# Graph layer with top-p attention: the first row tile of the second step is guessed from 24 of 26 key tiles, and the work around the turn is regrouped

## The chip, the cores and the metric

The kernel runs on one core of one Trainium2 chip. The metric is device time in microseconds of one execution; several runs are given by their median. A profiled execution is one run of the same program with the hardware profiler on, and all rows come from such a run.

## The reference

There are N = 3327 nodes with 256 features. After a layer norm and a ReLU the layer makes two steps of two diffusions. One goes through a sparse random adjacency matrix (about four entries a row besides the diagonal), the other through attention that keeps, in every row, the largest probabilities up to a mass of 0.9:

```python
h = jnp.maximum(_layernorm(x, axis=-1), 0.0)
# attention of one step
q = X @ W1.T @ W2.T
k = X @ W3.T
probs = jax.nn.softmax(q @ k.T / TAU, axis=-1)
idx = jnp.argsort(-probs, axis=-1)
sp = jnp.take_along_axis(probs, idx, axis=-1)
cs = jnp.cumsum(sp, axis=-1)
keep_sorted = cs - sp < TOP_P          # TOP_P = 0.9
A = probs * mask
A = A / jnp.maximum(A.sum(-1, keepdims=True), 1e-12)
# two steps; R is the row-normalised adjacency plus the identity
for n in range(2):
    A = _top_p_attention(Xa, W1, W2, W3)
    Xf = R @ Xf
    Xa = A @ Xa
    Z = Z + Xf @ U1[n].T + Xa @ U2[n].T
```

The result is a layer norm of `X + Z`, added to x. What matters here: the second step's keys are made from the first step's result, so no row of the second step can be summed over all columns before the last row tile of the first step is done.

## The kernel before

The rows are cut into 26 tiles of 128 (3328 with one padding row). For each row tile, `weights` takes the queries from `project`, multiplies them with all keys on TensorE (PE, `pl`, L603) in four chunks of 832 columns (two halves of 416), and ScalarE (ACT) writes the exponentials into one of a few buffers of 128 x 3328 (L607, the last chunk L611 and L613), with their sums in `za`. Nothing is sorted. Instead the threshold of each row is guessed and then settled from a few candidates:

- `guessed` (L619 to L629) computes a first threshold on ACT from the row's sum Z and from the moments of its logits (`ms`). In the first step and for tiles 0 to 2 of the second these come from `moments` (L507) and `project` (L519); for the other tiles of the second step `laws` (L553) makes them in one go: PE L561, VectorE (DVE) L564 to L568, and operations over 23 columns on GpSimd (POOL), L572 to L579.
- `measured_once` (first step) or `measured_twice` (second) measures mass and count at that threshold by scans over the whole row on ACT (`ja`, L636; three scans in the second step) and corrects it, with single columns computed on DVE (L688, L689, L702, L703, L719, L720), POOL (L680, L681, L693 to L695, L700 to L715) and ACT.
- `settle` makes, on DVE, the masked row `w` with the mass below the guess (L734), takes the 8 largest of each of 20 segments (`cand`, L739), draws the largest 48 in six rounds (`bb`, L746, L748), finds by cumulated sums (L753 to L758) the last one that is kept, and writes the masked exponentials back into `e` (L768; L765 in two pieces for tiles 0 and 25).
- `prove` (L776) checks for a whole step, in small DVE operations on 26 columns, that the guesses left the answer inside the candidates. If they did not, a flag sends the program through the slow `search_graph_layer` afterwards.

The masked row is then transposed by PE (`pt`, L813), copied by ACT (`eT`, L815) and multiplied with the features on PE (`pa`, L827); `finish` ends the tile.

The adjacency part is sparse: `refetch` gathers the rows of `vx`, the first step's result in DRAM, with five indirect DMAs a tile that POOL issues (L906, `xg<-vx`); each gather waits for all writes to `vx`. `spread` and `diffuse` multiply them on PE into `pr` (L914), a PSUM buffer of which there is one, and DVE ends it (L1087, L1088); in the first step it then writes `vx` for its tile.

The outer loop runs over tiles `i` in each step. In one turn each running piece of work (a Python generator) is advanced in an order written out by hand: seven parts a turn, each part a string of letters in which `m` is the guess of the next tile, `d` the settling of this one, `c` the end of the settling before it, `s` a spread, `g` a refetch, `l` the laws, `w` and `q` the logits and queries of later tiles, `f` finish and `e` the end of the first step. PE, ACT and DVE execute in exactly this text order from the first turn on, POOL from the start of the second step on:

```python
PLAN = (("mdsssa", "mdsssa", "edawwp", "msda", "mpdea", "gdawwq", "emdgq"),
        ("llcmss", "lnms", "lwwnfd", "lcmdsssg", "fmswqdf", "llmdf", "lmwfd"))
```

At the turn between the steps (`step == 1 and i == -1`) the kernel completes the logits of tile 0, proves the first step, makes all laws, measures tile 0, and refetches the adjacency rows of tiles 0 and 1, all before tile 0 is settled. `moments(1)` and three projections follow the first step's turn `i == NT`. The spreads of tiles 24 and 25 of the first step stand in its turns `i == NT` and `NT + 1`.

Of the kernel before, what the change touches and what calls it, by code (L numbers as in the profile page):

```python
# [9 lines left out]
F32 = mybir.dt.float32  # L10
# [318 lines left out]
HALVES = 9  # L329
FIRST = 8 * P  # L330
CUT = 4

# [12 lines left out]
def guess_graph_layer(ctx, tc, x, adj, w1t, w2t, w3t, u1t, u2t, ln_g, ln_b, out, flag):  # L345
# [207 lines left out]
    def laws(ts):  # L553

        at = lambda k, a, b: law[:, k, a:b]
        few_of = [ts[h::2][n : n + 3] for n in range(0, len(ts), 3) for h in range(2)]
        for few in filter(len, few_of):
            pq = ps_t.tile([P, 4, P], F32, tag="pt", name="pq")
            pm = pq.rearrange("p a b -> p (a b)")[:, : 3 * (2 * DA + 2)].rearrange("p (t n) -> p t n", t=3)
            for k, t in enumerate(few):  # L560
                PE.matmul(pm[:, k, :], query_of(t), qm[query_at(t), 1, :], start=True, stop=True)  # L561
            wide = scan.tile([P, NP], F32, tag="w", name="wide")
            mq = wide[:, : 3 * (2 * DA + 2)].rearrange("p (t n) -> p t n", t=3)
            V.tensor_copy(mq[:, : len(few)], pm[:, : len(few)])  # L564
            V.tensor_copy(law[:, 2, few[0] : few[-1] + 1 : 2], mq[:, : len(few), DA])
            for k, t in enumerate(few):
                V.scalar_tensor_tensor(mq[:, k, : DA + 1], mq[:, k, : DA + 1], 1.0, mq[:, k, DA + 1 :],
                                       ALU.mult, ALU.mult, accum_out=at(1, t, t + 1))  # L568
            yield
        a, b = ts[0], ts[-1] + 1  # L570
        s, var, m = (at(k, a, b) for k in range(3))
        G.tensor_tensor(s, var, halves[:, a:b], ALU.pow)  # L572
# [12 lines left out]
    def weights(step, t, live, known=True):  # L585

        r = dict(Z=rec[:, step, 3, t : t + 1])
        qT, r["ms"] = yield from project(step, t, law=known and not step)
        if known and step:
            r["ms"] = law_of(t)  # L590
        yield
        r["ms"] = r["ms"] or early.get(t)
        r["e"] = e = es[(2, 3, 0, 1, 4, 5)[t % 6] if step else t % 4]
        r["za"] = za = small.tile([P, CUT + 1], F32, tag="za", name="za")
        live[step, t] = r
        w = HALF * P
        wd = w // CUT
        for n in range(CUT):
            c = n * wd
# [6 lines left out]
            if n < CUT - 1:  # L606
                S.activation(e.rearrange("p (a n) -> p a n", a=2)[:, :, c : c + wd], pl[:, :, :wd],  # L607
                             AF.Exp, accum_out=za[:, n : n + 1])
                yield
            else:  # L610
                S.activation(e.rearrange("p (a n) -> p a n", a=2)[:, :, c : w - 1], pl[:, :, : wd - 1],  # L611
                             AF.Exp, accum_out=za[:, n : n + 1])
                S.activation(e[:, w - 1 : w], pl[:, 0, wd - 1 : wd], AF.Exp, accum_out=za[:, n + 1 :])  # L613

# [16 lines left out]
    def con(k):  # L631
        return one[:, k : k + 1]
# [39 lines left out]
    def measured_twice(r):  # L672
# [46 lines left out]
        V.tensor_scalar(col(6), d1, col(0), BIG, ALU.is_lt, ALU.mult)  # L719
        V.tensor_scalar(col(16), col(3), col(13), col(6), ALU.mult, ALU.add)  # L720

    def measured(step, r):
        return measured_twice(r) if step else measured_once(r)

# [50 lines left out]

    def prove(step):  # L776
        v8, t, tn, Z = (rec[:, step, k, :] for k in range(4))
        ok = small.tile([P, NT], F32, tag="cum", name="ok", bufs=1)
        o2 = small.tile([P, NT], F32, tag="dr", name="o2", bufs=1)
        V.tensor_tensor(ok, v8, t, ALU.is_lt)  # L780
        V.tensor_tensor(o2, tn, t, ALU.is_lt)
        V.tensor_tensor(ok, ok, o2, ALU.mult)
        for a, c, op in ((tn, 0.0, ALU.is_gt), (t, 0.5 * BIG, ALU.is_lt),
                         (Z, 1.0e-30, ALU.is_gt), (Z, BIG, ALU.is_lt)):
            V.scalar_tensor_tensor(ok, a, c, ok, op, ALU.mult)
        V.tensor_scalar(ok, ok, 0.5, None, ALU.is_lt)
        n = N - (NT - 1) * P
        f = small.tile([P, 1], F32, tag="f", name="f")
        V.tensor_reduce(f, ok[:, : NT - 1], AX.X, ALU.add)
        V.tensor_tensor(fl, fl, f, ALU.add)  # L790
        V.tensor_tensor(fl[:n], fl[:n], ok[:n, NT - 1 :], ALU.add)
        if step == 0:
# [3 lines left out]
            V.tensor_tensor(fl, fl, f, ALU.add)  # L796
# [173 lines left out]
    def run(work, n=99):  # L970
        for _ in range(n):
            next(work, None)
# [141 lines left out]
    for step in range(2):  # L1114
        sums = Sums(step, live, xw if step else x0, AHEAD[step])

        for i in range(-1, NT + 2):
# [26 lines left out]
            if step == 0 and i >= NT - 2 and i < NT + 1:  # L1144

                work["w"] = itertools.islice(begun[i - NT + 2], CUT - 1)
            if step == 0 and i >= NT - 3 and i < NT:
# [2 lines left out]
                work["w"] = itertools.chain(begun[1], begun[2])  # L1150
            if step == 0 and i < 1:
                work["b"] = itertools.islice(product, EARLY[i + 2] - EARLY[i + 1])
            if step == 1 and i == -1:
                work["g"] = itertools.chain(refetch(0), refetch(1))
            for k in range(PARTS):
                g = PARTS * (i - 1) + k - LATE[step]
                summing = valid(g // PARTS)
                if summing and step:
                    sums.turn(g, min(i, NT - 1))
                for c in "bb" + (LAST.get(i, PLAN[1]) if step else PLAN[0])[k]:  # L1160
# [9 lines left out]
            if step == 1 and i == -1:  # L1170
                run(work["m"])
            if step == 0 and i == -1:
                G.memset(es[2][:, N:NP], 0.0)
            for c in "lcnwqsepgb" if step else "dmwqsepgb":
# [55 lines left out]
```

## Time and profile before

| quantity | us |
|---|---|
| median of 3 runs | 1430.68 (1430.28 to 1431.4) |
| the profiled execution, whole | 1432.74 |
| its span, first to last instruction | 1431.0 |
| PE busy | 1280.6 (89%) |
| DVE busy | 1221.3 (85%) |
| ACT busy | 1106.3 (77%) |
| POOL busy | 985.9 (69%) |
| keys of the second step complete (ACT L497) | 781.69 |
| w of tile 0, second step, begins (DVE L734) | 802.99 |
| e of tile 0 begins (DVE L765) | 826.58 |
| e of tile 1 begins (DVE L768) | 851.06 |

The mean granted PE clock is 0.965 of full speed. Times in rows count from the span's start. In a row of a timeline the first number is the start, the second the duration in us, then engine, line of kernel.py, operation, result and operands with their shapes; in brackets the engine's idle time before it and what ended it. A row may hold several instructions (x10). In the chain of waits each row is a piece of the chain that ended last: start, duration, engine, result and line.

### The profile page before, as it was taken

How to read it: one execution, taken by the hardware profiler on the slowest of the kernel's cores; microseconds unless marked ns; L12 is line 12 of the kernel's file. 1: busy time of each engine (PE TensorE's matmuls, PEld its weight loads, DVE VectorE, ACT ScalarE, POOL GpSimd, SP SyncE). 2: the span in 40 equal slices, each digit the busy share in tenths (PEclk: the TensorE clock that was granted, in tenths of full speed). 3: DMA queues.
4: the chain of work that ended last, by engine and by line, in shares of the span. 5: the costliest groups of instructions: out<-in, count | busy, mean ns of one | idle time of the engine just before them, and what ended most of it. 6: DMA issues, size and time to landing. Idle time of an engine off the chain costs nothing.

```text
span 1431.0 us, 22249 instructions
## 1 busy us (share of the span) xinstructions
PE 1280.6 (89%) x6495; PEld 980.6 (69%) x6495; DVE 1221.3 (85%) x3724; ACT 1106.3 (77%) x2426; POOL 985.9 (69%) x1348
## 2 busy tenths in 40 slices
PE   6987799999999999999999469999999999999846
PEld 4534587777777777777777247777776777777745
DVE  5676999999999999998872589999999999999980
ACT  5358588787887878788844789999999999999811
POOL 6035477677676677678862667888878888888731
PEclk9998899999999999999999679999999999999978
DMA  7873445454454545433331212222122221221100
GB/s 248 291 245 93 123 124 152 125 148 131 141 143 129 144 130 146 137 103 78 99 89 52 66 38 78 71 63 89 57 77 74 61 89 55 79 78 56 56 8 22
DMA packets 91203, 149.78 MB, mean 105 GB/s; under 512 B 15265, under 2 KB 58656, under 8 KB 91072
## 3 DMA queue, kind: packets, MB, share of 16 engines
q1 hardware_dynamic: 73616, 105.37, 23.6%
q0 software_dynamic: 16640, 42.69, 11.7%
q8 instruction: 54, 0.88, 0.3%
q14 instruction: 77, 0.63, 0.1%
q10 hardware_dynamic: 816, 0.20, 0.1%
HBM read 120.93 MB, written 27.28 MB: 104 GB/s over the span
## 4 chain that ended last, share of the span: by engine, by line
DVE 50%; PE 24%; ACT 16%; POOL 4%; issue 4%; DMA 2%; SPq 0%; POOLq 0%; DVEq 0%; ACTq 0%
ACT ja L636 10%; PE pa L827 10%; DVE e L768 10%; DVE cand L739 7%; DVE w L734 6%; DVE fm L849 5%; PE pl L603 4%; DVE bb L746 4%; DVE cand L748 4%; PE pt L813 3%; DVE x L768 2%; PE pz L991 2%; ACT eT L815 2%; POOL xg L906 2%; PE pr L914 2%
## 5 line engine op out<-in xcount | busy, mean ns | idle before, releaser
L827 PE MATMUL pa<-xw,eT 128*128 128x256 f32 x1352 | 332.5, 388 | 18.6 <-DVE s L938 18.4
L636 ACT ACTIVATE ja<-e,g 128x3328 uint8<-128x3328 f32 x106 | 325.9, 3074 | 0.1
L827 PE MATMUL pa<-x,eT 128*128 128x256 f32 x1352 | 324.8, 382 | 0.0
L827 PEld LDWEIGHTS pa<-xw,eT 128*128 128x128 f32 x1352 | 250.4, 192 | 80.2 <-issue 27.1
L815 ACT COPY eT<-pt 128x512 f32<-128x512 f32 (+1 forms) x364 | 202.1, 556 | 104.7 <-PE pt L813 104.5
L827 PEld LDWEIGHTS pa<-x,eT 128*128 128x128 f32 x1352 | 244.8, 192 | 26.2
L739 DVE MAX8 cand<-w 128x8 f32<-128x168 f32 (+1 forms) x1040 | 251.0, 317 | 0.0
L813 PE MATMUL pt<-ident,e 128*128 128x128 f32 x1144 | 182.0, 280 | 68.8 <-DVE e L768 47.4
L906 POOL DMA_INDIRECT xg<-bx,index x130 | 194.8, 1498 | 48.5 <-issue 37.6
L813 PEld LDWEIGHTS pt<-ident,e 128*128 128x128 f32 x1144 | 141.7, 145 | 115.8 <-issue 55.9
L897 POOL DMA_INDIRECT ac<-in_adj,index x130 | 133.6, 1028 | 120.7 <-DVE ms L541 83.9
L734 DVE SCALAR_TENSOR_TENSOR w<-e,g 128x3328 f32<-128x3328 f32 x44 | 168.9, 3838 | 0.7
L906 POOL DMA_INDIRECT xg<-vx,index x130 | 130.9, 1007 | 45.6 <-issue 33.0
L768 DVE SCALAR_TENSOR_TENSOR e<-e,rec 128x3328 f32<-128x3328 f32 x40 | 155.7, 3891 | 0.7
L914 PE MATMUL pr<-xg,ac 128*128 128x257 f32 (+1 forms) x520 | 139.4, 392 | 12.1 <-DVE s L1088 12.0
L607 ACT ACTIVATE e<-pl 128x832 f32<-128x832 f32 x132 | 112.8, 858 | 32.4 <-PE pl L603 32.3
L914 PEld LDWEIGHTS pr<-xg,ac 128*128 128x128 f32 x520 | 94.0, 195 | 25.8 <-DVE s L1088 12.1
L954 POOL TENSOR_TENSOR s<-s,gam 128x256 f32<-128x256 f32 x25 | 92.5, 3699 | 9.0 <-ACT s L953 9.0
L746 DVE MAX8 bb<-cand 128x8 f32<-128x160 f32 x286 | 92.8, 325 | 6.4
L603 PE MATMUL pl<-both,qT 64*128 64x416 f32 x416 | 93.0, 551 | 5.3 <-ACT e L607 3.8
L603 PE MATMUL pl<-after,qT 64*128 64x416 f32 x416 | 96.7, 559 | 0.6 <-ACT qT L531 0.6
L770 POOL TENSOR_TENSOR cum<-dr,bb 128x48 f32<-128x48 f32 x26 | 84.8, 3261 | 15.1 <-DVE rec L758 15.0
(259 smaller groups left out, 2193.8 us busy)
## 6 DMA issues: line engine op xcount, KB each, us to landing
at<-in_adj SPq DMA_DIRECT2D x102, 256.0 KB, 2.7
cx<-ac SPq DMA_DIRECT2D x26, 384.0 KB
ac<-cx SPq DMA_DIRECT2D x26, 384.0 KB, 3.0
wide<-in_adj SPq DMA_DIRECT2D x10, 832.0 KB, 6.6
e<-in_adj SPq DMA_DIRECT2D x8, 832.0 KB
bx<-e SPq DMA_DIRECT2D x26, 128.5 KB, 3.8
own<-bx SPq DMA_DIRECT2D x26, 128.5 KB, 3.3
x<-in_x SPq DMA_DIRECT2D x13, 256.0 KB, 5.0
```

What stands on the lines that cost most here:

```text
L603: PE.matmul(pl[:, a, :wd], qT[p, :], keys_of(step, a).rearrange("p a b -> p (a b)")[:, c : c + wd], start=True, stop=True)
L636: S.activation(ja, e, f, bias=guess, scale=sign, accum_out=total)
L734: V.scalar_tensor_tensor(w, e, col(16), e, ALU.is_lt, ALU.mult, accum_out=d2)
L739: V.max(cand[:, 8 * s : 8 * s + 8], w[:, s * SEG : min(NP, (s + 1) * SEG)])
L746: V.max(b8, cand)
L768: V.scalar_tensor_tensor(e, e, at(1), e, ALU.is_ge, ALU.mult, accum_out=ra)
L813: PE.transpose(pt[:, j, :], e[:, (j0 + j) * P : (j0 + j + 1) * P], ident)
L815: S.copy(eT[:, :w, :], pt[:, :w, :])
L827: PE.matmul(self.pa, eT[:, c - 4 * k, :], self.xa[:, j, :], start=c == 0, stop=c == NT - 1)
L897: G.indirect_dma_start(out=ac[:, k, :], out_offset=None, in_=rows, in_offset=bass.IndirectOffsetOnAxis(ap=index[:, t, k : k + 1], axis=0), ...
L906: G.indirect_dma_start(out=xg[:, k, :w], out_offset=None, in_=rows, in_offset=bass.IndirectOffsetOnAxis(ap=index[:, t, k : k + 1], axis=0))
L914: PE.matmul(pr[:, :w], ac[:, k, :], own if k == KT - 1 else xg[:, k, :w], start=k == 0, stop=k == KT - 1)
```

## The change

The change concerns the end of the first step and the first turns of the second.

- In `weights`, tile 0 of the second step gets five chunks of columns for four: the fourth chunk is cut at `SEEN` = 12 x 128 in each half, that is at the columns of 24 of the 26 key tiles; the last 128 columns of each half are a chunk of their own.
- A new function `foreseen` takes the place of `measured_twice` for this tile. Its first threshold comes from the sum over the 24 tiles, scaled by NP / (2 SEEN). The mass and count at this threshold come from DVE: over 3072 columns first, over the other 256 later. The scan at the second threshold is halved: ACT takes one half of the row, DVE the other. Its single columns are computed on DVE and ACT, none on POOL.
- `moments(1)`, its three projections and the creation of `laws` stand after turn NT - 2 of the first step. The laws are made in small parts: two groups in turn NT, three in turn 0 of the second step, the rest and the POOL operations in turn 1. The copy that they need is 195 columns wide, was 390, and lies in another buffer.
- The spreads of tiles 24 and 25 of the first step stand after tile 0's `w` in the text.
- The logits of tile 2 (`begun[2]`) and the refetches of tiles 0, 1 and 2 stand in turn 0 of the second step; turn -1 holds nothing else any more.
- `prove(0)` stands after turn 1 of the second step, so that its instructions come just before `e` of tile 1 on DVE; it uses a row buffer in place of small ones.
- Turns NT and NT + 1 of the first step and turn 0 of the second get plans of their own (`TURN`, `OPEN`).

```diff
+SEEN = 12 * P
@@ laws
-            wide = scan.tile([P, NP], F32, tag="w", name="wide")
-            mq = wide[:, : 3 * (2 * DA + 2)].rearrange("p (t n) -> p t n", t=3)
-            V.tensor_copy(mq[:, : len(few)], pm[:, : len(few)])
-            V.tensor_copy(law[:, 2, few[0] : few[-1] + 1 : 2], mq[:, : len(few), DA])
+            mq = row.tile([P, D], F32, tag="xa", name="mq", bufs=2)
+            mq = mq[:, : 3 * (DA + 1)].rearrange("p (t n) -> p t n", t=3)
+            V.tensor_copy(mq[:, : len(few)], pm[:, : len(few), DA + 1 :])
+            V.tensor_copy(law[:, 2, few[0] : few[-1] + 1 : 2], pm[:, : len(few), DA])
@@ weights
+        ends_at = [w // CUT * n for n in range(1, CUT + 1)]
+        if (step, t) == (1, 0):
+            ends_at[CUT - 1 :] = [SEEN, w]
...
@@ new
+    def foreseen(r):
...
+        def count(part, f, guess, total):
+            n = part.shape[2]
+            wide = scan.tile([P, NP], F32, tag="w", name="wide")
+            out = wide[:, : 2 * n].rearrange("p (a n) -> p a n", a=2)
+            V.tensor_scalar(out, part, guess, None, f, ALU.add, accum_out=total)
+
+        S.activation(za[:, :CUT], za[:, :CUT], AF.Copy, accum_out=col(18))
+        S.activation(col(0), col(18), AF.Ln, scale=NP / (2 * SEEN))
...
+        count(seen, ALU.min, col(9), at(0))
+        yield
+        count(seen, ALU.is_ge, col(9), at(1))
+        V.tensor_scalar(col(11), col(11), ms(5), ms(6), ALU.mult, ALU.add)
+        yield
+        count(unseen, ALU.min, col(9), at(2))
+        count(unseen, ALU.is_ge, col(9), at(3))
...
+        S.activation(col(6), col(4), AF.Ln, scale=col(1), bias=con(2))
+        S.activation(col(6), col(6), AF.Exp, scale=col(11))
+        S.activation(col(13), col(6), AF.Copy, scale=col(9))
+        w = HALF * P
+        ja = scan.tile([P, NP], U8, tag="ja", name="ja")
+        S.activation(ja[:, :w], e[:, w:], AF.Sign, bias=col(13), scale=-1.0, accum_out=at(4))
+        V.tensor_scalar(col(5), at(1), -0.5 * w, None, ALU.add)
+        wide = scan.tile([P, NP], F32, tag="w", name="wide")
+        V.tensor_scalar(wide[:, :w], e[:, :w], col(13), None, ALU.is_ge, ALU.add, accum_out=at(5))
...
+        V.tensor_scalar(col(16), col(3), col(13), col(6), ALU.mult, ALU.add)
@@ prove
-        ok = small.tile([P, NT], F32, tag="cum", name="ok", bufs=1)
-        o2 = small.tile([P, NT], F32, tag="dr", name="o2", bufs=1)
+        pair = row.tile([P, D], F32, tag="xa", name="pair", bufs=2)
+        ok, o2 = pair[:, :NT], pair[:, NT : 2 * NT]
@@ the loop
+    TURN = {NT: ("yx", "", "ex", "", "ex", "l", "el"), NT + 1: ("", "e", "e", "e", "e", "", "")}
+    OPEN = ("mq", "mdg", "wldn", "mdwlg", "mdswl", "mdss", "mdsw")
...
             if step == 1 and i == -1:
                 run(begun[0])
-                prove(0)
+                run(ahead)
+                first = settle(1, 0, live[1, 0])
+                next(first)
+                run(begun[1])
+                for t in (NT - 2, NT - 1):
+                    run(spread(0, t))
                 for e in es[4:]:
                     G.memset(e[:, N:NP], 0.0)
+                continue
...
-                s=spread(step, i - 2 + 2 * step) if valid(i - 2 + 2 * step) else none,
+                s=spread(step, i - 2 + 2 * step) if valid(i - 2 + 2 * step) and step + NT > i else none,
...
-                l=laws(range(3, NT)) if step and i == -1 else none,
+                l=lawing if i in ((NT,), (0, 1))[step] else none, x=none, y=none,
             )
+            if step == 0 and i == NT:
+                ahead = foreseen(live[1, 0])
+                work.update(x=ahead, y=itertools.islice(begun[0], 1))
+            if step == 1 and i == 0:
+                work.update(d=first, w=begun[2], g=itertools.chain(refetch(0), refetch(1), refetch(2)))
...
-            if step == 1 and i == -1:
-                work["g"] = itertools.chain(refetch(0), refetch(1))
...
-            if step == 0 and i == NT:
+            if step == 0 and i == NT - 2:
                 moments(1, gsum)
                 for t in range(3):
-                    live[1, t]["ms"] = returned(project(1, t, queries=False))
+                    early[t] = returned(project(1, t, queries=False))
+                live[1, 0]["ms"] = early[0]
+                lawing = laws(range(3, NT))
+            if step == 1 and i == 1:
+                prove(0)
```

More of the change, by code (lines that the diff above doesn't have):

```diff
@@ L561, in laws @@
                 PE.matmul(pm[:, k, :], query_of(t), qm[query_at(t), 1, :], start=True, stop=True)
-            wide = scan.tile([P, NP], F32, tag="w", name="wide")
-            mq = wide[:, : 3 * (2 * DA + 2)].rearrange("p (t n) -> p t n", t=3)
-            V.tensor_copy(mq[:, : len(few)], pm[:, : len(few)])
-            V.tensor_copy(law[:, 2, few[0] : few[-1] + 1 : 2], mq[:, : len(few), DA])
+            mq = row.tile([P, D], F32, tag="xa", name="mq", bufs=2)
+            mq = mq[:, : 3 * (DA + 1)].rearrange("p (t n) -> p t n", t=3)
+            V.tensor_copy(mq[:, : len(few)], pm[:, : len(few), DA + 1 :])
+            V.tensor_copy(law[:, 2, few[0] : few[-1] + 1 : 2], pm[:, : len(few), DA])
             for k, t in enumerate(few):
-                V.scalar_tensor_tensor(mq[:, k, : DA + 1], mq[:, k, : DA + 1], 1.0, mq[:, k, DA + 1 :],
-                                       ALU.mult, ALU.mult, accum_out=at(1, t, t + 1))
+                V.scalar_tensor_tensor(mq[:, k], pm[:, k, : DA + 1], 1.0, mq[:, k], ALU.mult, ALU.mult,
+                                       accum_out=at(1, t, t + 1))
             yield
@@ L593, in weights @@
         r["e"] = e = es[(2, 3, 0, 1, 4, 5)[t % 6] if step else t % 4]
-        r["za"] = za = small.tile([P, CUT + 1], F32, tag="za", name="za")
+        w = HALF * P
+        ends_at = [w // CUT * n for n in range(1, CUT + 1)]
+        if (step, t) == (1, 0):
+            ends_at[CUT - 1 :] = [SEEN, w]
+        za = small.tile([P, CUT + 2], F32, tag="za", name="za")
+        r["za"] = za[:, : len(ends_at) + 1]
         live[step, t] = r
[L596 to L599, printed above, removed]
+        for n, (c, end) in enumerate(zip([0] + ends_at, ends_at)):
+            wd = end - c
             pl = ps_l.tile([P, 2, 512], F32, tag="pl", name="pl")
@@ L605, in weights @@
                           start=True, stop=True)
-            if n < CUT - 1:
+            if end < w:
                 S.activation(e.rearrange("p (a n) -> p a n", a=2)[:, :, c : c + wd], pl[:, :, :wd],
@@ L612, in weights @@
                              AF.Exp, accum_out=za[:, n : n + 1])
-                S.activation(e[:, w - 1 : w], pl[:, 0, wd - 1 : wd], AF.Exp, accum_out=za[:, n + 1 :])
+                S.activation(e[:, w - 1 : w], pl[:, 0, wd - 1 : wd], AF.Exp, accum_out=za[:, n + 1 : n + 2])
     def guessed(r, g):
@@ L720, in measured_twice @@
         V.tensor_scalar(col(16), col(3), col(13), col(6), ALU.mult, ALU.add)
+    def foreseen(r):
+        e, ms, za, Z = r["e"], r["ms"], r["za"], r["Z"]
+        both_of = e.rearrange("p (a n) -> p a n", a=2)
+        seen, unseen = both_of[:, :, :SEEN], both_of[:, :, SEEN:]
+        r["col"] = col = lambda k, g=small.tile([P, 19], F32, tag="g0", name="g0", bufs=1): g[:, k : k + 1]
+        s = small.tile([P, 6], F32, tag="s6", name="s6", bufs=1)
+        at = lambda k: s[:, k : k + 1]
+        def count(part, f, guess, total):
[5 more added lines that the diff above has]
+        S.activation(col(0), col(18), AF.Ln, scale=NP / (2 * SEEN))
+        S.activation(col(2), col(0), AF.Relu, scale=-0.25, bias=ms(7))
+        S.activation(col(2), col(2), AF.Exp, scale=-1.0, bias=con(6))
+        S.activation(col(3), col(2), AF.Square, bias=con(3))
+        S.activation(col(9), col(3), AF.Exp, scale=ms(3), bias=ms(8))
+        S.activation(col(11), col(2), AF.Square, bias=con(4))
+        yield
[3 more added lines that the diff above has]
+        V.tensor_scalar(col(11), col(11), ms(5), ms(6), ALU.mult, ALU.add)
+        yield
+        count(unseen, ALU.min, col(9), at(2))
+        count(unseen, ALU.is_ge, col(9), at(3))
+        V.tensor_reduce(Z, za, AX.X, ALU.add)
+        V.tensor_tensor(s[:, :2], s[:, :2], s[:, 2:4], ALU.add)
+        V.reciprocal(col(1), Z)
+        V.tensor_scalar(col(4), at(1), col(9), -1.0, ALU.mult, ALU.mult)
+        V.tensor_scalar(col(4), col(4), at(0), None, ALU.add)
+        V.tensor_scalar(col(1), col(1), 10.0, None, ALU.mult)
+        S.activation(col(6), col(4), AF.Ln, scale=col(1), bias=con(2))
+        S.activation(col(6), col(6), AF.Exp, scale=col(11))
+        S.activation(col(13), col(6), AF.Copy, scale=col(9))
+        w = HALF * P
+        ja = scan.tile([P, NP], U8, tag="ja", name="ja")
[3 more added lines that the diff above has]
+        V.tensor_scalar(wide[:, :w], e[:, :w], col(13), None, ALU.is_ge, ALU.add, accum_out=at(5))
+        V.tensor_scalar(col(14), col(13), col(9), 0.5, ALU.add, ALU.mult)
+        V.tensor_scalar(at(2), at(4), -0.5, at(5), ALU.mult, ALU.add)
+        V.tensor_scalar(col(15), col(5), at(2), col(14), ALU.subtract, ALU.mult)
+        d1 = col(17)
+        V.tensor_scalar(d1, col(15), col(4), 0.0, ALU.add, ALU.max)
+        V.tensor_scalar(col(10), col(13), col(1), OFFSET[1], ALU.mult, ALU.mult)
+        V.tensor_scalar(col(10), col(10), 1.0, None, ALU.add)
+        S.activation(col(2), d1, AF.Abs, scale=col(1), bias=con(1))
+        S.activation(col(3), d1, AF.Ln, scale=col(1), bias=con(2))
+        S.activation(col(2), col(2), AF.Ln, scale=0.2, bias=col(10))
+        S.activation(col(2), col(2), AF.Identity, scale=-1.0, bias=col(3))
+        V.tensor_scalar(col(8), col(4), col(1), -1.0, ALU.mult, ALU.mult)
+        V.tensor_scalar(col(12), col(4), d1, col(1), ALU.subtract, ALU.mult)
+        V.tensor_scalar(col(8), col(8), 1.0, col(12), ALU.add, ALU.mult)
+        V.tensor_scalar(col(12), col(12), col(12), 1.0e-12, ALU.mult, ALU.add)
+        V.reciprocal(col(12), col(12))
+        V.tensor_scalar(col(12), col(12), col(8), 0.7, ALU.mult, ALU.max)
+        V.tensor_scalar(col(11), col(12), 1.5, col(11), ALU.min, ALU.mult)
+        S.activation(col(3), col(2), AF.Exp, scale=col(11))
+        V.tensor_scalar(col(0), at(2), 30.5 - 0.5 * w, BIG, ALU.is_lt, ALU.mult)
+        V.tensor_scalar(col(5), Z, 0.035, col(0), ALU.mult, ALU.add)
+        V.tensor_scalar(col(6), d1, col(5), BIG, ALU.is_lt, ALU.mult)
+        V.tensor_scalar(col(16), col(3), col(13), col(6), ALU.mult, ALU.add)
@@ L1143, in guess_graph_layer @@
                 work["q"] = itertools.islice(later[step, i + 3], 2 - step)
-            if step == 0 and i >= NT - 2 and i < NT + 1:
+            if step == 0 and i >= NT - 2 and i < NT:
                 work["w"] = itertools.islice(begun[i - NT + 2], CUT - 1)
@@ L1159, in guess_graph_layer @@
                     sums.turn(g, min(i, NT - 1))
-                for c in "bb" + (LAST.get(i, PLAN[1]) if step else PLAN[0])[k]:
+                for c in "bb" + (LAST.get(i, PLAN[1] if i else OPEN) if step else TURN.get(i, PLAN[0]))[k]:
                     next(work[c], None)
@@ L1169, in guess_graph_layer @@
                         work["f"] = finish(ended[0], live.pop(("f", ended[0])), *ended[1])
-            if step == 1 and i == -1:
-                run(work["m"])
             if step == 0 and i == -1:
                 G.memset(es[2][:, N:NP], 0.0)
+            if step and i == 0:
+                work["l"] = none
             for c in "lcnwqsepgb" if step else "dmwqsepgb":
                 run(work[c])
-            if step == 0 and i == NT:
+            if step == 0 and i == NT - 2:
                 moments(1, gsum)
                 for t in range(3):
-                    live[1, t]["ms"] = returned(project(1, t, queries=False))
+                    early[t] = returned(project(1, t, queries=False))
[3 more added lines that the diff above has]
+                prove(0)
     run(work["f"])
```

## The prediction

> **What bounds the kernel now.** I began with the page's slices of the span (each 35.8 us; digits are tenths busy).
>
> ```profile
> PE   6987799999999999999999469999999999999846
> DVE  5676999999999999998872589999999999999980
> ACT  5358588787887878788844789999999999999811
> PEclk9998899999999999999999679999999999999978
> ```
>
> The first step runs against PE, the second against PE and DVE together; between them, slices 23 and 24, nothing is full and PE's clock drops. The change works only there, so the question is what the hole of some 60 us (787 to 848) consists of, and how much earlier the second step's cycle comes out of it. The chain of waits gives the hole in order (start, us, engine, result, line):
>
> ```profile
> 782.46 0.95 ACT e L611 x2
> ...
> 802.32 4.01 POOL law L572
> ...
> 809.68 1.13 POOL xg L906
> ...
> 822.86 0.28 POOL g L693
> ...
> 823.16 0.28 DVE g L702
> ...
> 851.06 3.70 DVE e L768 x2
> ...
> 854.90 0.63 PE pt L813 x4
> ...
> 872.88 4.09 DVE e L768 x2
> ...
> 895.16 4.01 DVE e L768 x2
> ```
>
> The last keys end at 781.69; ACT then guesses tile 0's threshold with three whole scans. From 802.3 to 823.1 the chain is POOL's queue: the seven law operations, then ten gathers with tile 1's column (L693) behind them. From 851.06 on the masking product e follows e by 21.8 and 22.3 us: that cycle (e, transposes, eT, scan, columns, bb rounds, next e) runs unbroken to the end. **What the change is worth is therefore one number: how far e of tile 1, at 851.06, moves.** An earlier e of tile 0 alone is worth nothing. The timelines of DVE and POOL show the rows that I price with:
>
> ```profile
> 778.25 0.18 DVE L780 TENSOR_TENSOR ok<-rec 128x26 f32<-128x26 f32 x1
> ...
> 781.18 0.16 DVE L796 TENSOR_TENSOR fl<-fl,f 128x1 f32<-128x1 f32 x1
> ...
> 802.99 3.68 DVE L734 SCALAR_TENSOR_TENSOR w<-e,g 128x3328 f32<-128x3328 f32 x1
> ...
> 826.58 1.29 DVE L765 SCALAR_TENSOR_TENSOR e<-e,rec 128x1024 f32<-128x1024 f32 x1
> ...
> 847.65 0.27 DVE L702 TENSOR_SCALAR g<-oa,g 128x1 f32<-128x1 f32 x1 [4.40 <-ACT ja L636]
> ```
>
> ```profile
> 787.12 1.08 POOL L906 DMA_INDIRECT xg<-vx,index  x1 [0.28 <-issue]
> ...
> 802.29 4.04 POOL L572 TENSOR_TENSOR law<-law,halves 128x23 f32<-128x23 f32 x1
> ...
> 831.47 4.53 POOL L906 DMA_INDIRECT xg<-vx,index  x1 [0.28 <-issue]
> ```
>
> The gathers of tile 0 began at 787.12, each 0.95 us every 1.25. One of 4.53 us stands beside DVE's w of tile 1 (831.33 to 835.0): a gather issued under such a two-input pass waits it out, +3.6 us. L702 of tile 2 at 847.65 waited for ACT's scan; from there a fixed run of rows (three bb rounds, cum, dr) leads to e(1) 3.41 us later.
>
> **The change, part by part,** on the times of the profiled execution (1432.74, span 1431.0; it lies 2.06 above the median 1430.68, so shifts are added to the median).
>
> *Tail of the first step, PE-bound.* Out of PE's way before the last keys: spread of tile 24, 2.61 (750.15 to 751.46 and 752.76 to 754.06); the logits of tile 2, 2.50 (1.60 at 756.54, 0.90 at 766.50); moments and projections, 2.21 (771.67 to 773.88); spread of tile 25, about 2.3 (its own 2.70 and most of the idle 0.65 before L927, less ACT's copy of xa, now exposed). Into it: the moments two tiles earlier, 2.21 and a wait of about 1.0 for POOL's gsum (729.02 to 729.35); 288 columns of logits 0.62; two groups of law matmuls at 0.42; about 0.85 of eT copies behind the guess's small ACT operations. Sum -9.6 + 5.5: the keys end 4 us earlier, near 777.4.
>
> *Tile 0's guess.* Before, 21.6 us from keys to w (781.4 to 802.99). After: last exps 0.8, two counts over 256 columns 0.95, six small DVE operations 1.15, three ACT 1.15 (L690 to L692), the half scans 2.0, ten small operations and one exp 3.9, hand-overs 0.5. Sum 10.5: w at 787.9, 15.1 us earlier. The one-input counts have no row: the two lengths of L765 (1.29 at 1024, 2.61 at 2304) give 1.03 ns a column as a ceiling (2.0 for 1664), half as a floor. I take the ceiling; on the path it is 1 us either way. Counts over 3072 columns run while the keys are made.
>
> *The moved spreads.* This is what the diff hides. Both now stand behind w in DVE's order, and pr has one buffer (ps_r): PE makes pr(24), then waits for DVE's L1088 of tile 24, queued behind w, until about 792.5. It has idled 11.5 us; in such stretches the trace shows half clock (0.50 from 806 on; eight logit passes 3.15 at 817.09 against 1.67 at 756.54). So pr(25), 2.7 when warm (1.40 and 1.30 from 773.88 and 776.15) and 5.4 at half clock throughout, is taken at 4.9 and ends at 797.4; DVE stands still for it 5 us before the first cand, and PE's pq of tile 3 and ACT's scans of tile 1 are queued behind it. The Trainium skill (TensorE: Matmul & The Clock Gate, Part 1) says that an idle window of some 3.4 us halves the clock and a like busy time restores it; that rule speaks against this change, and by it pr(25) would be cold for its first 3.4 us only, 4.4 in all by an estimate, which would make the sum +0.2. vx of tile 25 is then written at 798.1, not 778.36; a write lands 2.5 us later (1.8 to 3.2), and every refetch gather waits for all of vx. POOL's first gather moves from 787.12 to 800.9, and the ten end at 813.2.
>
> *What that makes of POOL.* cand, bb and e of tile 0 follow on DVE (e 812.6 to 816.5, before 826.58); POOL's columns of tile 1 end at 821.0, so w(1) starts at 823.05, 8.3 us earlier. POOL then issues tile 2's five gathers (821.2, one held by w(1): 831.35), two columns, the laws (802.29 to 809.19 before: 6.9; to 838.6), tile 3's gathers (839 to 845.0), and only then tile 2's column L693. ACT's three scans of tile 2 would allow L702(2) at 842.15, 5.5 us earlier; POOL allows it at 845.3: -2.35.
>
> *prove.* Its 15 DVE operations (778.25 to 781.34, 3.05 us) lay beside PE's tail; behind them only the keys' work stood. Now they stand directly before e of tile 1, with all of DVE serial from L702 on: +3.05, nothing hides it. The smaller law copies (195 columns for 390, 0.56 each before) and the repeated row buffer cost nothing here: DVE has idle time beside them.
>
> **Sum:** e(1) at 845.3 + 3.41 + 3.05 = 851.8 against 851.06: **+0.7 us, no measurable change** (0.2%, 2.9 us, is what a measurement of this kernel can tell). The cycle passes that shift on to the end: 1430.68 + 0.7 = 1431.4.
>
> Open prices: vx landing -0.7 to +0.7; laws 6.9 to 7.3; a last gather held by e of tile 0, 0 or +3.6; pr(25) warm or wholly cold, -2.2 to +0.5. The Trainium skill (GPSIMD Engine Reference, Specifications) says that POOL shares its SBUF interfaces with DVE and contends with its two-input instructions; the row of 4.53 agrees, and the rule would hold a gather under every w and e, the +3.6 case, 1435.0.
>
> **The rivals.** *A: faster.* POOL has tile 2's column in time. It needs 3.2 us: no gather held by w of tile 1 (-3.6) is enough, or a warm pr(25) (-2.2) with an early landing (-0.7) and half of the counts' ceiling (-1). Then ACT decides: -5.5 + 3.05 = -2.45, still not measurable; but what brings pr(25) earlier also frees ACT's queue, up to another 3 us, so down to -5.5: 1425.2. For it: the hole is mostly waiting, and w(0) gains 15 us. Against: POOL's rows leave little slack, and prove is certain.
>
> *B: slower.* POOL's queue as the price of vx written 20 us late. It decides once L693(2) comes after 847.4 (e(1) above 853.9): +0.7, the held gather 3.6, landing 0.7, laws 0.4 make +5.4, 1436.1. For it: the chain shows just this queue as the bound of the hole today. Against: the gather of 4.53 needs an exact overlap.
>
> *C: it does not do what it says.* If the scaled sum over 24 tiles guesses badly, a row's candidates fail and the whole search runs again, hundreds of us at least. Working the guess through on the given inputs, I find at most 20 of the 48 candidates used in tile 0, so I leave 1%.
>
> **How the numbers follow.** Forecast within 0.2%: 0.40. A beyond -2.9: 0.26. B beyond +2.9 with C: 0.34; B is ahead of A, since both unpriced waits (gather held, ACT queue behind PE) can more easily grow than vanish. Range 1425.2 to 1436.1: A's end to B's end; it leaves out about 2 in 10, half of it C and longer waits. The likeliest case's own range is 1428 to 1433.5.
>
> **What would show it.** In the changed profile: keys done near 777; w of tile 0 near 788; a PE hole of about 11 us ahead of pr(25), which then runs at half clock; DVE idle 5 us before the first cand; first vx gather near 801; the laws on POOL between two sets of gathers; the prove rows directly before e of tile 1; that e near 852. It is wrong if pr(25) runs before w, if tile 2's column on POOL does not hold L702, or if the step from one e to the next after tile 1 differs from 22.2.

## The result, and the profile after

The changed kernel takes 1441.95 us (median of 4 runs, 1440.7 to 1444.01) against 1430.48 before: ratio 1.0081, interval 1.0063 to 1.0098, 0.8% slower and outside the forecast range. The profiled execution took 1441.54 with a span of 1439.7, 8.7 over the span before. The difference of 11.5 us between the medians is larger, because the profiled execution before lay 2.3 us above its median and the one after 0.4 below; what the other runs add to the 8.7 no trace shows.

The page's slices of the changed kernel:

```profile
PE   6987799999999999999997669999999999999856
DVE  6676999999999999998864768999999999999980
ACT  5358588787877888787944668999999999999811
PEclk9998899999999999999999679999999999999978
```

In slice 22 PE has 7 where it had 9. In slices 23 and 24 PE has 6 6 where it had 4 6, but ACT goes from 7 8 to 6 6, DVE from 5 8 to 7 6, and both reach only 8 in slice 25, where they had 9: the hole begins earlier, is filled a little more, and lasts longer. The chain of waits says where it went (start, us, engine, result, line; up to the scans on ACT lines are 1 to 4 higher than before, from `settle` on 72):

```profile
782.34 0.27 ACT after L497
...
796.95 4.50 PE pr L986 x12
801.68 0.50 DVE s L1160
802.20 3.33 DMA vx<-s
...
806.35 1.02 POOL xg L978
...
835.98 4.06 POOL law L573
...
849.49 0.28 POOL g L697
849.79 0.29 DVE g L706
...
856.14 3.62 DVE e L840 x2
859.89 1.08 PE pt L885 x4
860.97 3.08 PE pl L607 x8
```

From 797 to 849 it is the spread of tile 25, the write of vx, and POOL's queue. On DVE and POOL:

```profile
792.32 3.69 DVE L806 SCALAR_TENSOR_TENSOR w<-e,g 128x3328 f32<-128x3328 f32 x1
...
849.79 0.27 DVE L706 TENSOR_SCALAR g<-oa,g 128x1 f32<-128x1 f32 x1 [9.75 <-POOL g L697]
...
853.09 0.18 DVE L852 TENSOR_TENSOR pair<-rec 128x26 f32<-128x26 f32 x1
...
856.06 3.67 DVE L840 SCALAR_TENSOR_TENSOR e<-e,rec 128x3328 f32<-128x3328 f32 x1
```

```profile
815.19 1.82 POOL L978 DMA_INDIRECT xg<-vx,index  x1 [0.30 <-issue]
817.32 2.24 POOL L978 DMA_INDIRECT xg<-vx,index  x1 [0.30 <-issue]
...
827.06 4.38 POOL L978 DMA_INDIRECT xg<-vx,index  x1 [0.31 <-issue]
```

w of tile 0 begins 9.7 us after the last keys (782.62), where it was 21.6: the guess does what it says. But DVE then waits 9.75 us for one column of POOL, prove follows, and e of tile 1 starts at 856.06 instead of 851.06.

The start of the program differs by up to 3 us between executions, so I compare stretches of the traces between four landmarks, from one profiled run each: **A**, ACT's last copy of the keys of tile 22; **B**, that of tile 25; **C**, e of tile 1; **D**, e of tile 2, from where the cycle is 22.2 to 22.3 us in every run of the table.

| run | A to B | B to C | C to D | A to D |
|---|---|---|---|---|
| before | 55.5 | 69.6 | 21.8 | 147.0 |
| changed | 55.9 | 73.4 | 24.3 | 153.7 |
| prove early (e1) | 57.4 | 71.2 | 24.3 | 152.9 |
| spreads in the guess (e2) | 54.3 | 64.9 | 23.3 | 142.4 |
| moments later (e3) | 53.0 | 73.7 | 24.4 | 151.1 |
| before, prove late (e4) | 55.5 | 72.3 | 24.5 | 152.4 |
| PE kept busy (e9) | 55.9 | 73.9 | 21.8 | 151.7 |
| before, moments early (e11) | 58.1 | 69.0 | 21.8 | 148.9 |
| laws in two (e10) | 54.7 | 58.0 | 22.3 | 135.0 |

For the changed kernel this is 6.7 us up to D (0.4, 3.8 and 2.5). Ahead of A lie 0.8 us. Another 1.3 come at the last tile, where a group of sums runs at half clock. Before and after:

```profile
1352.22 1.99 PE L827 MATMUL pa<-xw,eT 128*128 128x256 f32 x8 [2.48 <-DVE s L938]
```

```profile
1359.86 3.59 PE L899 MATMUL pa<-xw,eT 128*128 128x256 f32 x8 [2.49 <-DVE s L1010]
```

PE's wait ahead of this group is 2.48 or 2.49 us in all thirteen traces of this document; the group took 1.99 us in three of them (before, e2, e11) and 3.10 to 3.68 in ten (e4, the kernel before but for the place of `prove`, among them). So the 1.3 us are the clock's, and whether the new order has a part in them is not shown.

### The profile page after: what moved, and what is told of

Its sections match the earlier page's. It is cut to its first block, busy times and chain, and to the rows that moved or that the text cites. A ratio compares the mean times of both kernels' runs of the same rounds, so it can differ in the third digit from the quotient of the medians.

```text
span 1439.7 us, 22260 instructions
## 1 busy us (share of the span) xinstructions
PE 1287.0 (89%) x6499; PEld 983.0 (68%) x6499; DVE 1230.3 (85%) x3753; ACT 1099.6 (76%) x2423; POOL 981.8 (68%) x1335
## 4 chain that ended last, share of the span: by engine, by line
DVE 48%; PE 23%; ACT 15%; POOL 5%; issue 5%; DMA 3%; SPq 0%; POOLq 0%; DVEq 0%; ACTq 0%
PE pa L899 10%; DVE e L840 9%; ACT ja L640 9%; DVE cand L811 7%; DVE w L806 5%; DVE fm L921 5%; PE pl L607 4%; DVE bb L818 4%; DVE cand L820 4%; PE pt L885 3%; POOL xg L978 3%; DVE x L840 2%; PE pz L1063 2%; ACT eT L887 2%; PE pr L986 2%
## 5 line engine op out<-in xcount | busy, mean ns | idle before, releaser
L640 ACT ACTIVATE ja<-e,g 128x3328 uint8<-128x3328 f32 x103 | 316.7, 3074 | 0.0
L969 POOL DMA_INDIRECT ac<-in_adj,index x130 | 130.3, 1002 | 115.7 <-DVE ms L542 79.5
L986 PE MATMUL pr<-xg,ac 128*128 128x257 f32 (+1 forms) x520 | 141.3, 396 | 17.6 <-issue 10.3
L611 ACT ACTIVATE e<-pl 128x832 f32<-128x832 f32 (+1 forms) x133 | 113.6, 857 | 31.7 <-PE pl L607 31.6
L607 PE MATMUL pl<-after,qT 64*128 64x416 f32 (+1 forms) x420 | 99.5, 569 | 0.2 <-ACT after L497 0.2
L842 POOL TENSOR_TENSOR cum<-dr,bb 128x48 f32<-128x48 f32 x26 | 79.1, 3042 | 15.0 <-DVE rec L830 15.0
```

The costliest lines, as they stand in the source:

```text
L607: PE.matmul(pl[:, a, :wd], qT[p, :], keys_of(step, a).rearrange("p a b -> p (a b)")[:, c : c + wd], start=True, stop=True)
L640: S.activation(ja, e, f, bias=guess, scale=sign, accum_out=total)
L969: G.indirect_dma_start(out=ac[:, k, :], out_offset=None, in_=rows, in_offset=bass.IndirectOffsetOnAxis(ap=index[:, t, k : k + 1], axis=0), ...
L986: PE.matmul(pr[:, :w], ac[:, k, :], own if k == KT - 1 else xg[:, k, :w], start=k == 0, stop=k == KT - 1)
```

## The experiments

**The parts of the change, one by one.** Prove placed ahead of the column of tile 2 on DVE:

```diff
+                if step == 1 and i == 1 and k == 6:
+                    prove(0)
...
-            if step == 1 and i == 1:
-                prove(0)
```

> The changed kernel with prove(0) ahead of the column L706 of tile 2 on DVE, in the 9.75 us in which DVE there waits for POOL, instead of directly before e of tile 1. Theory (prove stands on the cycle, and the 7.44 us that PE waits for e leave it at half clock, which costs another 2.5 us up to e of tile 2): e of tile 1 3.0 us earlier, at about 853, PE's wait for it about 4.4, the step from there to the next e 21.8 in place of 24.3, so 5 to 5.6 us faster than the changed kernel: about 1436. Rival (prove costs only its own rows; the cold clock has another cause): 3.0 faster, about 1438.5. Rival (the end is set elsewhere): within 1 us of 1441.5.

Measured: ratio to before 1.0045 (1.0032 to 1.0058), 1438.0 us beside 1432.2. In the trace prove begins at 839.05, inside DVE's wait, and the way from L706 to e of tile 1 is 3.42 us where it was 6.27: those 2.85 us were prove's, as said. The step from C to D stayed at 24.3 us: that half of the theory fell in this form, for PE still waited 4.33 us for e and ran cold after it (at half clock: the four transposes took 1.09 us). By the medians this kernel is 5.8 us over its own runs of before, where the change was 11.5 over its own, so it seems to gain more than the 2.3 us from B to C; but the two pairs come from different rounds, and of the 3.7 us between the two profiled runs 3.0 lie ahead of A, where the two kernels do the same.

The spreads:

```diff
         V.tensor_scalar(col(5), at(1), -0.5 * w, None, ALU.add)
+        yield
...
+                next(ahead)
+                run(spread(0, NT - 2))
                 run(ahead)
+                run(spread(0, NT - 1))
                 first = settle(1, 0, live[1, 0])
                 next(first)
                 run(begun[1])
-                for t in (NT - 2, NT - 1):
-                    run(spread(0, t))
```

> The changed kernel with the DVE ends of the spreads of tiles 24 and 25 inside the guess of tile 0 (the first ahead of the half scan on DVE, the second just before w) instead of behind w. Theory (the late write of vx, 802.2, and through it POOL's queue of gathers sets e of tile 1): w of tile 0 1.3 us later, pr(25) warm and without the wait of 10.3 us, vx of tile 25 written near 793, first gather near 797 instead of 806.35, column L697 of tile 2 some 6 to 9 us earlier, e of tile 1 6 to 9 us earlier, so about 1433 to 1436. Rival (ACT's scans or the gathers held by DVE's passes set e of tile 1, not vx): 0 to 3 us faster, 1439 to 1442.

Measured: 0.9996 (0.9988 to 1.0005), the whole loss gone. Rows of this kernel on PE, POOL and DVE:

```profile
783.05 2.41 PE L987 MATMUL pr<-xg,ac 128*128 128x257 f32 x10 [0.83 <-PE pr L987]
```

```profile
793.55 1.02 POOL L979 DMA_INDIRECT xg<-vx,index  x1 [0.27 <-issue]
```

```profile
837.53 0.27 DVE L706 TENSOR_SCALAR g<-oa,g 128x1 f32<-128x1 f32 x1 [8.49 <-POOL g L697]
...
843.80 3.67 DVE L841 SCALAR_TENSOR_TENSOR e<-e,rec 128x3328 f32<-128x3328 f32 x1
```

pr(25) starts 0.83 us after PE is done with the other, not 10.3, and runs warm; the first gather comes 14.7 us after the keys instead of 23.7, and e of tile 1 8.5 us earlier, counted from B. Two DVE instructions behind w, for a tile of the first step, cost that much. POOL still decides: DVE waits 8.49 us for its column. The profiled run of this kernel lay 4.9 us under the median of its twelve, so the 4.6 us that the table gives it over before are no gain of the medians.

Moments one tile later:

```diff
-            if step == 0 and i == NT - 2:
+            if step == 0 and i == NT - 1:
                 moments(1, gsum)
...
-                live[1, 0]["ms"] = early[0]
+                for t in range(2):
+                    live[1, t]["ms"] = early[t]
```

> The changed kernel with moments and the three projections one tile later in the first step (after turn NT - 1 instead of NT - 2). Theory (at their place PE waits 1.0 us for POOL's sum, and the idle time leaves PE at half clock for the next passes, 1.9 us more; one tile later the sum has long been there): the keys of the second step 1 to 3 us earlier than 782.88, and the end as much earlier, about 1439 to 1440.5. Rival (the tail is lengthened elsewhere, by ACT's small operations between the transposes): no change, 1441.5 within 1 us, or slower if the law columns now come too late for the guess.

Measured: 1.0050 (1.0037 to 1.0063); A to B 53.0 instead of 55.9, 2.9 us as the theory had it. The same part put alone into the kernel before:

```diff
-            if step == 0 and i == NT:
+            if step == 0 and i == NT - 2:
                 moments(1, gsum)
...
```

> The kernel before with one part of the change: moments and its three projections two tiles earlier in the first step. Theory (PE waits there for POOL's sum and for the copies, and runs the next passes at half clock): the stretch from the keys of tile 22 to those of tile 23 grows from 22.6 by 4 to 6 us, the turn gives back the 2.2 us of the old place: 2 to 4 us slower than before. Rival (the half clock belongs to the guess of tile 0, which is not in this kernel): the stretch grows by 3.3 at most, 0 to 1 us slower.

Measured: 1.0015 (1.0006 to 1.0025), 2.45 us slower between the medians. Its PE rows:

```profile
729.38 0.40 PE L512 MATMUL pq<-gs,w2x 64*128 64x65 f32 x2 [1.01 <-DVE gs L510]
730.32 0.49 PE L528 MATMUL pq<-qm,both 64*128 64x130 f32 x4 [0.54 <-DVE qm L516]
731.13 0.49 PE L528 MATMUL pq<-qm,both 64*128 64x130 f32 x2 [0.32 <-ACT mq L535]
731.55 2.25 PE L914 MATMUL pr<-xg,ac 128*128 128x257 f32 x6
```

The three waits are 1.87 us together, and the six passes behind them take 2.25 us where 1.57 is warm. From the keys of tile 22 to those of tile 23 it is 27.5 us here and in the changed kernel, 22.6 before. In the six traces with moments at this place the stretch is 25.8 (e2, e9), 27.5 (these two) or 29.0 us (e1, e5). The waits are the same each time; what the clock makes of them is not: in e2 and e9 the six passes take 1.57 us, at a granted clock of 1.00, in the changed kernel 2.83, at 0.51, in e1 and e5 2.94.

Prove alone, late, in the kernel before (with the row buffer that the change gives it):

```diff
                 run(begun[0])
-                prove(0)
...
+            if step == 1 and i == 1:
+                prove(0)
```

> The kernel before with one part of the change: prove(0) taken from the turn and put directly before e of tile 1. Theory (3.05 us on the cycle, and PE's wait for e grows from 0.64 to 3.7 us, so that its clock may drop): e of tile 1 at about 854, 3.0 to 5.5 us slower than before, 1433.5 to 1436. Rival (the turn is shortened by as much, because prove stood on the path to the keys): no change, 1430.5.

Measured: 1.0046 (1.0034 to 1.0059), 6.9 us between the medians, 5.4 from A to D: 2.7 up to e of tile 1 and 2.7 behind it. PE had waited 3.48 us for that e (0.64 before):

```profile
858.24 1.08 PE L813 MATMUL pt<-ident,e 128*128 128x128 f32 x4 [3.48 <-DVE e L768]
859.25 3.15 PE L603 MATMUL pl<-after,qT 64*128 64x416 f32 x8
```

Four transposes take 1.08 us instead of 0.63, eight logit passes 3.15 instead of 1.67. So a delay of 2.7 us on DVE became one of 5.4, by the clock (0.50 between 858 and 862 us).

**The clock by itself.** PE gets work in the wait ahead of e of tile 1, 28 matmuls of two passes each:

```diff
+                if self.step and self.turned == PARTS:
+                    idle = ps_t.tile([P, 4, P], F32, tag="pt", name="idle")
+                    for _ in range(28):
+                        PE.matmul(idle[:, 0, :], ident, ident, start=True, stop=True)
```

> The changed kernel with 28 matmuls of 128 columns more on PE, whose result nothing reads, just ahead of the transposes of e of tile 1 in PE's order (about 6 us, in the 7.4 us in which PE waits for that e). Theory (PE's wait lets its clock fall to half, and the transposes, logits and sums of the next cycle run cold, 24.3 us from e of tile 1 to the next e in place of 21.8): with PE kept busy the clock stays up, the step is 21.8 to 22.2, e of tile 1 itself does not move, and the end comes 2 to 2.5 us earlier than the changed kernel's. Rival (the 24.3 us has another cause, a late column or scan): the step stays at 24.3 or grows.

Measured: 1.0045 (1.0032 to 1.0058). On PE:

```profile
853.93 6.52 PE L885 MATMUL idle<-ident 128*128 128x128 f32 x56 [0.55 <-ACT eT L891]
860.57 0.63 PE L889 MATMUL pt<-ident,e 128*128 128x128 f32 x4
861.13 1.67 PE L607 MATMUL pl<-after,qT 64*128 64x416 f32 x8
```

Compare the changed kernel, where PE idled 7.44 us:

```profile
859.89 1.08 PE L885 MATMUL pt<-ident,e 128*128 128x128 f32 x4 [7.44 <-DVE e L840]
860.90 3.15 PE L607 MATMUL pl<-after,qT 64*128 64x416 f32 x8
```

e of tile 1 stayed where it was and the step behind it fell from 24.3 to 21.80 us: work that nobody reads is worth 2.5 us here. Between 860 and 864 us the granted clock is 1.00 here and 0.50 in the changed kernel. That shows the cause of the slow step.

**Toward a better order.** Four kernels ran on one chip whose runs of the kernel before spread from 1432.6 to 1450.3, so their intervals are wide. The change as it is:

> The changed kernel as it is, run beside the others on one chip, as their measure: 8 to 12 us over the kernel before. In its trace the stretch from the keys of tile 21 to those of tile 23 in the first step (27.5 us, against 22.6 before) varies by a few us from run to run if the half clock after moments comes from a clock window that runs freely; the steps after the keys repeat to within 1 us.

Measured: 1.0092 (1.0060 to 1.0125); keys of tile 22 to 23 29.0 us (the stretch of 27.5 in the expectation, which names tile 21), B to C 74.0 and C to D 24.6, as said. All three displacements undone:

> The changed kernel with all three displacements undone: the spreads inside the guess, prove ahead of the column of tile 2, moments one tile later. Theory (three independent costs): in the trace with the spreads alone DVE still waits 8.5 us for that column, so prove's 3.05 us are hidden there; the keys come 3 to 5 us earlier; together 6 to 8 us below the kernel with the spreads alone, at 1424 to 1426, and 6 to 8 us faster than before. Rival (the displacements are alternatives to each other, e of tile 1 being set by something common): 1430 to 1432, no better than the spreads alone.

Measured: 0.9988 (0.9962 to 1.0014), not the 6 to 8 us. B to C is 63.7: prove is hidden, but POOL's column comes 1.6 us later after the keys than with the spreads alone, and DVE still waits 5.62 for it: the rival was half right, POOL is the common bound. Then POOL's laws behind the columns of tile 2 (turn 1 gets a plan of its own, with its last `l` at the end):

```diff
+    THEN = ("llcmss", "lnms", "wwnfd", "cmdsssg", "fmswqdf", "mdf", "mwfdl")
...
```

> As the kernel with all three, and POOL's seven law operations (6.9 us) moved behind the columns of tile 2 instead of ahead of the gathers of tile 3. Theory (POOL's queue still sets the column L697 of tile 2): DVE's wait for it falls from 8.5 us towards 1.5 to 3, prove (3.05) comes out of its cover in part, e of tile 1 3 to 5 us earlier, 1420 to 1423. Rival (ACT's third scan of tile 2 ends at about the same time): no change against the kernel with all three. Rival (the laws now come too late for the guess of tile 3): e of tile 2 later, slower than the kernel with all three.

Measured: 0.9963 (0.9938 to 0.9989), 5 us faster than before between the medians, less than expected. B to C falls to 58.7, as expected, and C to D grows to 27.3: the last rival came true as well. ACT's guess of tile 3 waited for the laws:

```profile
857.05 0.29 ACT L629 ACTIVATE g<-g,law 128x1 f32<-128x1 f32 x1 [6.22 <-POOL law L580]
```

And a shorter wait of PE, for e of tile 2, was enough for half clock, 0.50 from 882 to 884 us:

```profile
881.96 1.08 PE L886 MATMUL pt<-ident,e 128*128 128x128 f32 x4 [2.39 <-DVE e L841]
```

Prove in the wait for the last keys on top of that:

```diff
+                if step == 0 and i == NT + 1 and k == 1:
+                    prove(0)
```

> As the kernel with the laws later, but prove in the 7 us in which DVE waits for the last keys (776.4 to 783.8 in the changed kernel's trace). Theory (with the column of tile 2 in time, prove is on the cycle again where it stands): 2 to 3 us faster than the kernel with the laws later, 1418 to 1420. Rival (DVE still waits there, for ACT's scan): no difference, or slower by up to 1 us where prove touches the count of the last columns.

Measured: 0.9991 (0.9958 to 1.0024), no gain shown, and B to C is 59.8 us, 1.1 longer: DVE waited 4.45 us for ACT's scan at the column of tile 2, which covers prove in either place, as the rival said. Last, the laws of tiles 3 to 8 early and the other columns late:

```diff
...
+            if n == 1:
+                settled(ts[0], ts[6])
             yield
-        a, b = ts[0], ts[-1] + 1
+        settled(ts[6], ts[-1] + 1)
+
+    def settled(a, b):
```

> Spreads inside the guess, moments one tile later, prove in the wait for the last keys, and the POOL part of the laws in two: tiles 3 to 8 right after their two groups, while POOL waits for vx, the other 17 columns behind the columns of tile 2. Theory (in the kernel with the laws later the step from e of tile 1 to the next was 27.3 us because tile 3's guess waited for POOL's laws until 857; without that it is 22 to 24): from the last keys to e of tile 1 about 58 us (before: 69.6), to e of tile 2 about 81 (before: 91.5), the keys 2.5 us earlier, so 10 to 13 us faster than the kernel before. Rival (another column, or ACT's scans, takes over as the bound): 5 to 8 us faster, no better than the kernel with the laws later.

Measured: **0.9921 (0.9908 to 0.9934), 1421.57 us beside 1432.52**, 11 us faster than before, with 58.0 and 80.3 us from the keys to C and D as expected, though the keys came only 0.9 earlier. Its POOL and PE:

```profile
774.71 1.37 POOL L578 TENSOR_TENSOR law<-law,halves 128x6 f32<-128x6 f32 x1 [6.05 <-DVE mq L568]
...
795.48 1.10 POOL L984 DMA_INDIRECT xg<-vx,index  x1 [0.28 <-issue]
...
838.73 3.08 POOL L578 TENSOR_TENSOR law<-law,halves 128x17 f32<-128x17 f32 x1
```

```profile
842.71 0.63 PE L891 MATMUL pt<-ident,e 128*128 128x128 f32 x4 [0.67 <-DVE e L846]
```

The first laws stand in POOL's wait for vx, the others behind the columns that DVE needs; PE waits 0.67 us for e of tile 1 and stays warm. The early guess itself computes in this kernel what it did.

## Why the prediction was wrong

The structure held: the end is set by e of tile 1, POOL's queue holds the column of tile 2, pr(25) waits behind w, prove stands on the cycle. Two steps of the sum failed: the keys that should end 4 us earlier, and the shift that the cycle should pass on to the end unchanged.

At e of tile 1 the sum gave +0.7 and the profiled runs +5.0 us. Between the two stand the keys (4.4 us) and the 0.8 ahead of A, less 1.0 by which the stretch from the keys to e of tile 1 was shorter than forecast (73.4 us; 851.8 less 777.4 are 74.4). Behind e of tile 1 come the 2.5 and the 1.3 of the last tile, for which the sum had no term. The remaining 2.8 us of the 11.5 stand between the profiled runs and their medians.

- *"The keys end 4 us earlier"* failed, the largest error: they end 0.4 later from A. Moments at 3.2 were 4.9 up to the keys of tile 23, the difference of 1.7 being cold passes (e11, e3), which two traces with moments at the same place escaped (e2, e9). In e2, which stays warm all the way, the keys are still only 1.2 us earlier. One cause is the stall behind the guess on ACT, 2.1, not 0.85 (in e9 it was PE's clock behind this stall that fell, to 0.51):

```profile
760.70 1.99 PE L899 MATMUL pa<-x,eT 128*128 128x256 f32 x8 [2.09 <-ACT xa L908]
```

The gains of the last stretch were smaller too: 3.3 from tile 24's keys to tile 25's, where 4.1 were counted.

- *"The cycle passes that shift on to the end"* failed: +2.5 us, the cold step behind e of tile 1 (e4 and e9 show it). The forecast's own sign of being wrong, a step that differs from 22.2 us, came true here with 24.3. I had priced half clock for pr(25) and not asked how long PE would wait for e. Tile 0 is ready 12 us earlier, so PE finishes its sums and idles. Speeding up one tile without the next can so be a loss.
- *vx and the gathers*: from w to the first gather 14.0 us, predicted 13.0, since vx landed in 3.33 instead of 2.5; the ten gathers took 14.5, not 12.3, two being held by the two pieces of e of tile 0. That was the open price "a last gather held", taken at its low end. Neither shows at e of tile 1, because POOL then began tile 2's gathers 4.8 us after the ten, where the forecast had 8.0, and the guess took less: errors that cancel, which is luck.
- *Rival B* met its own condition (L697 at 849.49, its point was 847.4), and its +5.4 is near the measured +5.0. That nearness is luck as well: its terms were a held gather, a late landing and the laws, behind keys that end early; what was measured are mostly the keys.
- *Right*: the guess 10.5 (9.7 measured), pr(25) 4.9 (4.5), from POOL's first gather of tile 2 over the laws to the column of tile 2 23.8 (23.9), L706 to e with prove 6.46 (6.27).

Of the two rules that the prediction took from the Trainium skill, that of GPSIMD Engine Reference, Specifications, agrees with this trace: the gathers under w and e took 4.38, 2.24 and 1.82 us instead of 0.95. The other, of TensorE: Matmul & The Clock Gate, Part 1, gives 4.4 us for pr(25) by an estimate, 4.50 measured, and its idle window of some 3.4 us fits the waits of 3.48, 4.33 and 7.44 (cold) and 0.67 (warm). Shorter waits do not fit it: those around moments, 1.87 us in all, cooled PE in four traces of six, 2.39 us did in e7, and 2.48 at the last tile in ten of thirteen. There the measurements decide.

What stays open: why the same waits cool PE in one trace and not in another, so that moments cost 3.3 to 6.4 us and the last tile 1.3 or nothing; why the keys gain only 1.2 us even in e2, of which the stall on ACT and the smaller gain at the end explain a part; and how much of the 11 us that the last kernel gains is the guess's own, since no run has its order with the old guess.

## What to carry to other kernels

Before moving work, list every instruction that ends up behind a long one on its engine, and follow each to the queue that waits for it, however small it is: here two DVE instructions behind w held a DRAM table, ten gathers and another tile's column. When one stage is made earlier, ask what its successor's engine does with the time: here PE paid again after waits of 3.5 us and more, and sometimes after shorter ones. Check the stretch ahead of the stage too, since the largest part of the forecast's error lay there. Judge a new algorithm only once the order around it is mended, since the same guess was part of a kernel that lost 11 us in one order and of one that gained 11 in another.

## What the runs showed of the hardware

- Matmuls that nobody reads, put into PE's wait, shorten the next cycle from 24.3 to 21.80 us.
- Three waits of 1.01, 0.54 and 0.32 us with short matmuls between them lowered PE's clock in four traces of six; six passes then took 2.25 to 2.94 us instead of 1.57.
- One wait of 2.48 us ahead of eight passes left them at 1.99 us in three traces and made them 3.10 to 3.68 in ten.
- The power operation on POOL over 23 columns took 4.05 us, over 17 columns 3.08 and over 6 columns 1.37.
